# Folding the squares of two scan directions into one 128-row tile, in a bidirectional Mamba-2 layer with a feed-forward part

## The chip, the cores and the metric

The kernel runs on one core of one Trainium2 chip, in float32 throughout. The metric is the device time of one execution in microseconds (us). Five engines work side by side, each through its own queue in order: TensorE (PE; its weight loads are listed apart as PEld), VectorE (DVE), ScalarE (ACT), GpSimd (POOL) and SyncE (SP), which issues the DMAs.

## What is computed

Eight sequences of 512 tokens with 256 channels. Each is normalised, run through a Mamba-2 block forward and another one backward, projected and added to the input; then it is normalised again and goes through a dense layer with a low-rank correction. The part that matters here is the end of each Mamba-2 block, the gate, the mean of squares over the 512 inner channels of a token, and the output projection:

```python
def _mamba2(x, Win, convw, convb, dtb, Alog, Dsk, normw, Wout):
    ...
    y = jnp.transpose(ys, (1, 0, 2, 3)) + Dsk[None, None, :, None] * xs
    y = y.reshape(b, l, D_INNER)
    y = y * _silu(z)
    y = y * jax.lax.rsqrt(jnp.mean(y * y, axis=-1, keepdims=True) + 1e-05) * normw
    return y @ Wout
...
out_fwd = _mamba2(x, fWin, ...)
out_rev = jnp.flip(_mamba2(jnp.flip(x, axis=1), bWin, ...), axis=1)
out = jnp.concatenate([out_fwd, out_rev], axis=-1) @ Wo + bo
```

## The kernel before

**Tiling.** A sequence `b` (0 to 7) is cut into four chunks of 128 tokens. A `Pair(b, c)` works on two chunks at once: chunk `c` for the forward direction (`d` = 0) and chunk 3 - `c` for the backward one (`d` = 1). Channels lie on the 128 partitions, so a gated output `yg` of one direction is a tile of 128 partitions x 4 blocks x 128 tokens.

**The main loop** (L942 to L1123) makes one pass for each pair, 32 in all; the text calls them pass (b, c). In a pass `p` is the pair whose outputs are made, `q` the next pair, which is prepared, and `before` the one before. A pass also does convolution blocks of a later sequence (`work`, at most four), gates of a later pair (`gate`, `gate_silu`), and the output projection and feed-forward part (`Tail`, one a pass as a rule) of chunks that are complete. The order in which each engine does all this is written out by hand: at the end of each pass `pin()` fixes the instructions of every engine in the order in which they were issued. A wait in one queue therefore holds up everything behind it in that queue.

**One pass**, as far as the steps of the change are concerned:

- GpSimd: the scaling of the state (`decay_state`, L625), the scaling of the next pair's decays (`scale_c`, L558), `times_gate` for both directions (L676), four times `scale_x` (L591), two bias additions (L757, L719), `norm_power` (L696), and then `presum` (L702, L703), which adds the four blocks of squares of both directions down to one.
- ScalarE: the copies of the transposed inputs (`turn`, L582), `norm2` (L748), `tap` (L424), the copy in the tail's `turn` (L764), `norm_mean` of the pair before (L690), `square` for both directions (L679), in some passes `norm1` (L256), a late `silu` (L449), the gate's first `silu` (L501), `skip` (L615), more silus, the second `tap`, and the gate's second `silu`.
- TensorE: `outputs` (L635), `add_state` (L655), `turn` (L580), a `project` of `work` (L413), the tail's transposes (L762), `norm_sum` of the pair before (L685), half a gate (L493), `cb` (L601), `ffn` (L769), the output projection (L731), and more of L413 and L493.
- VectorE: `evict` (L669), `new_state` (L664), four scans (L569), `convolve` (L431), `mix` (L607), `add_ffn` (L772), `residual` (L738) and statistics (L225, L226).

In pass (1, 2), (3, 2) and (5, 2) VectorE also works out the step sizes of two sequences to come (class `Steps`, L333 to L358).

**The squares.** `square` writes the squares of one direction over that direction's gates in the tile `sz` (partitions x direction x block x half x tokens). `presum` adds blocks 2 and 3 to 0 and 1, then block 1 to 0. In the next pass `norm_sum` transposes the remaining 128 x 128 square of each direction on TensorE, so that tokens come to the partitions, and `norm_mean` sums along the 128 channels that are left, with a scaled and biased activation that accumulates; `norm_power` turns the two columns into the inverse root. The slots of the PSUM pools `p_tr` (two) and `p_proj` (three) go round in the order of use: the result of `norm_sum` and both results of `cb` are in `p_tr`.

In the last pass of a sequence (c = 3, `hold` in the code) the order differs: `norm_sum` comes between the two `turn`s, and ScalarE copies the second `turn` after `norm_mean`.

Of the kernel before, what the change touches and what calls it, by code (L numbers as in the profile page):

```python
# [8 lines left out]
F32 = mybir.dt.float32  # L9
AF = mybir.ActivationFunctionType  # L10
ALU = mybir.AluOpType
# [3 lines left out]
P = 128  # L15
NB, L, DM = 8, 512, 256
NC = L // P
DI = 512
# [8 lines left out]
EPS = 1e-5  # L27
# [4 lines left out]
def tile_bimamba_ffn(  # L32
# [39 lines left out]
    pe, dve, act, pool, sp = nc.tensor, nc.vector, nc.scalar, nc.gpsimd, nc.sync  # L72

    const = ctx.enter_context(tc.tile_pool(name="const", bufs=1))
# [13 lines left out]
    def ps(p, shape, name):  # L88
        return p.tile(shape, F32, name=name, tag=p.name)
# [60 lines left out]
    ident = const.tile([P, P], F32, name="ident")  # L150
# [3 lines left out]
    pool.memset(zeros, 0.0)  # L154
    neghalf = const.tile([P, NC], F32, name="neghalf")
    pool.memset(neghalf, -0.5)
    eps_col = const.tile([P, 1], F32, name="eps_col")
    pool.memset(eps_col, EPS / P)

    upto = const.tile([P, P + 1], F32, name="upto")  # L160
    pool.memset(upto, 1.0)
# [109 lines left out]
    def sm(name, b0, shape=(P, P), bufs=1):  # L271
        return small.tile(list(shape), F32, name=f"{name}_{b0}", tag=name, bufs=bufs)
# [103 lines left out]
    def steps_last(b0):  # L376
        g = seq[b0]["g"]
        last = g["last"] = sm("last", b0, (P, 64))
        act.activation(last[F], fold[F], AF.Copy, scale=upto[F, P:])
        act.activation(last[W], fold[W], AF.Copy, scale=onward[W, 0:1])  # L380
# [137 lines left out]
    class Pair:  # L518


        def __init__(self, b, c):
# [5 lines left out]
            self.r0 = [d * 64 + (n * NSG + self.s["i"]) * NH for d, n in enumerate(self.cn)]  # L527
            self.xdt, self.xw = {}, {}

        def tile(self, tag, shape, bufs=2, d=""):  # L530
            return chp.tile(list(shape), F32, name=f"{tag}_{self.name}_{d}", tag=tag, bufs=bufs)

# [143 lines left out]
            pool.tensor_tensor(yg, yg, m.gates(d), ALU.mult)  # L676

        def square(m, d):
            act.activation(m.gates(d), m.s["yg", d, m.cn[d]], AF.Square)  # L679

        def norm_sum(m):

            m.ss = ps(p_tr, [P, 2, P], f"ss_{m.name}")
            for d in range(2):
                pe.transpose(m.ss[:, d, :], m.gates(d)[:, 0, :], ident)  # L685

        def norm_mean(m):
            m.rs = small.tile([P, 2], F32, name=f"rms_{m.name}", tag="rms", bufs=8)
            for d in range(2):
                act.activation(  # L690
                    m.ss[:, d, :], m.ss[:, d, :], AF.Identity, bias=eps_col[:, 0:1], scale=1.0 / DI,
                    accum_out=m.rs[:, d:d + 1],
                )

        def norm_power(m):
# [2 lines left out]
                m.s["rs", d, m.cn[d]] = m.rs[:, d:d + 1]  # L698

        def presum(m):  # L700
            sq = m.s["gates", m.c // 2].sz[:, :, :, m.c % 2, :]
            pool.tensor_tensor(sq[:, :, :2], sq[:, :, :2], sq[:, :, 2:], ALU.add)  # L702
            pool.tensor_tensor(sq[:, :, 0], sq[:, :, 0], sq[:, :, 1], ALU.add)  # L703

    class Tail:

# [163 lines left out]
    gates = Gates(0, 0)  # L870
# [46 lines left out]
    def when(t, *what):  # L917
        for one in t if isinstance(t, list) else [t]:
            if one is not None:
                for w in what:  # L920
                    if w:
                        getattr(one, w)()
# [19 lines left out]
    for i in range(n):  # L942
        p, q = pairs[i], pairs.get(i + 1)
        b, c = order[i]
        t, t0 = begun(i), begun(i - 1)
        gates = None

        def gate(j):
            nonlocal gates
            if gates is None:  # L950
                gates = gated(i)
            if j < len(gates):
                gates[j][0](*gates[j][2:])

        def gate_silu(j):
            if j < len(gates):
                gates[j][1](*gates[j][2:])
# [50 lines left out]
        when(t0, "turn")  # L1008
        if not hold:
            when(before, "norm_sum", "norm_mean")  # L1010
        for d in range(2):
            p.square(d)
        if even and c in (1, 3) and ahead < NB:
            norm1(ahead + (c == 3))
        if not hold and b:
# [3 lines left out]
        if q:  # L1019
            if not hold or work[0] is not None:  # L1020
                gate(0)
            q.cb()
            gate_silu(0)
            if i == 0:
                steps_last(0)
            for d in range(2):
                q.scale_x(d)
        when(t0, "bias2")
# [154 lines left out]
```

## Time and profile before

| | us |
|---|---|
| three runs: lowest, median, highest | 618.14, 620.36, 621.55 |
| the profiled execution, its own time | 619.29 |
| its span, from the first to the last instruction | 617.5 |
| pass (1, 0), the first that the change touches, starts at | 119.43 |
| pass (6, 3), the last whose squares it touches, starts at | 533.34 |
| pass (7, 0) starts at | 546.87 |

All times inside the profile count from the start of the span. The profile adds up, for each engine, how long it was busy, follows the chain of work that ended last back from the end, and lists groups of instructions by line, each with its count, total and mean. A group's line also tells how long the engine was idle before these instructions and what ended the wait. TensorE's matmuls overlap, so its busy share says little; how far apart they start says more. The granted clock of TensorE is 0.993 of full speed over the span.

### The profile page before, as it was taken

Reading aid. Unit: us, or ns where it says so; the run is one execution under the profiler, and the core shown is the slowest. Engines: PE = TensorE matmul, PEld = TensorE weight load, DVE = VectorE, ACT = ScalarE, POOL = GpSimd, SP = SyncE. Lnnn points to the kernel's source line nnn. Section 1 sums busy time; section 2 is a strip of 40 time slices with the busy share of each in tenths; the row PEclk is TensorE's granted clock in tenths of the full one; section 3 lists DMA queues with packets and bytes.
Section 4 is the critical chain, followed back from the end, with each engine's and each line's share of the span. In section 5 each row is a group of like instructions: output and inputs, shape, how many; then the busy total and the mean of one; then the engine's idle time right before and its main releaser. Section 6 shows DMA issues by size and latency. Waiting matters only on the chain.

```text
span 617.5 us, 11937 instructions
## 1 busy us (share of the span) xinstructions
PE 596.7 (97%) x4316; PEld 428.3 (69%) x4316; DVE 545.9 (88%) x826; ACT 412.2 (67%) x949; POOL 460.9 (75%) x559
## 2 busy tenths in 40 slices
PE   5989999999999999999999999999999999999996
PEld 2467677677676776766767677767767767777784
DVE  5887988889999989988999998888999998888963
ACT  3688786867676576785786766775877755565531
POOL 3287885777857897776859799677967889499972
PEclk9999999999999999999999999999999999999998
DMA  7475340026064423108026422305206442444011
GB/s 223 139 227 197 111 106 7 2 83 192 4 197 153 120 86 102 37 5 257 19 84 186 129 73 86 121 20 189 54 6 191 120 120 87 121 120 120 18 52 35
DMA packets 36250, 64.80 MB, mean 105 GB/s; under 512 B 8608, under 2 KB 23392, under 8 KB 36192
## 3 DMA queue, kind: packets, MB, share of 16 engines
q1 hardware_dynamic: 34048, 64.00, 34.1%
q8 instruction: 34, 0.56, 0.4%
q10 hardware_dynamic: 2144, 0.04, 0.2%
q14 instruction: 24, 0.20, 0.1%
HBM read 59.12 MB, written 4.72 MB: 103 GB/s over the span
## 4 chain that ended last, share of the span: by engine, by line
PE 65%; DVE 19%; ACT 6%; POOL 5%; issue 3%; DMA 2%; SPq 0%; DVEq 0%; POOLq 0%; ACTq 0%
PE pp L413 16%; PE pm L731 12%; PE pz L493 12%; PE py L635 9%; DVE lam L569 5%; DVE xc L431 4%; PE pf L769 4%; PE pxs L580 4%; PE pst L655 2%; DVE lam L607 2%; DVE yg L669 1%; PE cb L601 1%; DVE x L738 1%; PE pz L510 1%; DMA dec__1431<-dec 1%
## 5 line engine op out<-in xcount | busy, mean ns | idle before, releaser
L431 DVE SCALAR_TENSOR_TENSOR xc<-pp,conv_sb,xc 128x511 f32<-128x511 f32 x180 | 133.4, 744 | 25.9 <-ACT xc L424 21.7
L413 PE MATMUL pp<-xhT,win_sb 128*128 128x512 f32 x320 | 151.5, 600 | 1.0 <-ACT v L278 0.5
L569 DVE TENSOR_TENSOR_SCAN lam<-lam,seed 128x512 f32<-128x512 f32 x128 | 145.6, 1197 | 0.0
L676 POOL TENSOR_TENSOR yg<-yg,sz 128x512 f32<-128x512 f32 x64 | 80.8, 1284 | 57.5 <-DVE yg L669 49.4
L731 PE MATMUL pm<-wy,yg 128*128 128x256 f32 x512 | 115.8, 379 | 0.0
L493 PE MATMUL pz<-xhT,win_sb 128*128 128x256 f32 x448 | 106.5, 380 | 0.3 <-DVE xc L431 0.2
L731 PEld LDWEIGHTS pm<-wy,yg 128*128 128x128 f32 x512 | 97.0, 190 | 13.4 <-issue 0.3
L493 PEld LDWEIGHTS pz<-xhT,win_sb 128*128 128x128 f32 x448 | 82.4, 190 | 17.9 <-issue 4.5
L413 PEld LDWEIGHTS pp<-xhT,win_sb 128*128 128x128 f32 x320 | 57.9, 192 | 47.1 <-issue 42.5
L615 ACT ACTIVATE yg<-xc,dcol 128x128 f32<-128x128 f32 x256 | 81.0, 393 | 0.0
L424 ACT ACTIVATE xc<-pp,conv_sb 128x512 f32<-128x512 f32 x64 | 49.7, 779 | 43.3 <-PE pp L413 43.2
L607 DVE TENSOR_TENSOR lam<-lam,cb 128x1024 f32<-128x1024 f32 x64 | 74.9, 1211 | 1.7 <-PE cb L601 1.7
L591 POOL TENSOR_TENSOR xdt<-xs,dw 128x512 f32<-128x512 f32 x64 | 66.6, 1045 | 1.1 <-ACT xs L582 1.1
L635 PE MATMUL py<-lam,xdt 128*64 128x128 f32 x1024 | 63.0, 276 | 0.6 <-POOL xs L591 0.6
L582 ACT COPY xs<-pxs 128x512 f32<-128x512 f32 x64 | 35.1, 588 | 39.8 <-PE pxs L580 39.8
L635 PEld LDWEIGHTS py<-lam,xdt 128*64 128x64 f32 x1024 | 55.3, 137 | 8.8 <-issue 2.5
L501 ACT ACTIVATE sz<-pz 128x512 f32<-128x512 f32 x56 | 33.1, 591 | 32.1 <-PE pz L493 31.9
L591 POOL TENSOR_TENSOR xs<-xs,dw 128x512 f32<-128x512 f32 x48 | 50.2, 1045 | 3.8
L669 DVE TENSOR_TENSOR yg<-py,yg 128x512 f32<-128x512 f32 x64 | 41.5, 682 | 9.2 <-PE py L635 5.0
L580 PEld LDWEIGHTS pxs<-ident,xc 128*128 128x128 f32 x256 | 28.2, 141 | 26.8 <-issue 13.4
L679 ACT ACTIVATE sz<-yg 128x512 f32<-128x512 f32 x64 | 38.0, 627 | 9.5 <-POOL yg L676 9.4
L702 POOL TENSOR_TENSOR sz<-sz 128x512 f32<-128x512 f32 x32 | 40.8, 1276 | 0.3 <-ACT sz L679 0.3
(234 smaller groups left out, 944.8 us busy)
## 6 DMA issues: line engine op xcount, KB each, us to landing
lam<-dat SPq DMA_DIRECT2D x64, 512.0 KB
x<-in_x_dram SPq DMA_DIRECT2D x36, 128.0 KB
out_dram<-x SPq DMA_DIRECT2D x32, 128.0 KB
x<-in_x_dram SPq DMA_DIRECT2D x7, 512.0 KB
win_sb<-in_win_dram SPq DMA_DIRECT2D x2, 640.0 KB
win_sb<-in_win_dram SPq DMA_DIRECT2D x2, 512.0 KB
wot<-in_wout_t_dram SPq DMA_DIRECT2D x2, 512.0 KB
v<-raw SPq DMA_DIRECT2D x48, 4.0 KB
```

What stands on the lines that cost most here:

```text
L413: pe.matmul(pp, lhsT=win_sb[:, d, k, c0:c0 + P], rhs=s["xhT"][:, k, :], start=(k == 0), stop=(k == NK - 1),)
L424: act.activation(self.acc, self.pp, AF.Identity, bias=self.w[:, 4:5], scale=self.w[:, 3:4])
L431: dve.scalar_tensor_tensor(self.acc[:, to], self.pp[:, of], self.w[:, 3 - j:4 - j], self.acc[:, to], ALU.mult, ALU.add,)
L493: pe.matmul(pz[:, j, :], lhsT=win_sb[:, d, k, blk * P:(blk + 1) * P], rhs=self.s["xhT"][:, k, cols], start=(k == 0), stop=(k == NK - 1),)
L569: dve.tensor_tensor_scan(lam, lam, sd, 0.0, ALU.mult, ALU.add)
L580: pe.transpose(pt[:, blk * P:(blk + 1) * P], m.s["xc", d][:, blk, m.tcol[d]], ident)
L591: pool.tensor_tensor(hb(to), hb(m.xw[d]), dw[:, j, cols].unsqueeze(2).to_broadcast([P, NH, HD]), ALU.mult)
L607: dve.tensor_tensor(m.lam[d], m.lam[d], m.pcb[d].unsqueeze(1).to_broadcast([P, NH, P]), ALU.mult)
L615: act.activation(yg[:, blk, :], m.s["xc", d][:, blk, m.tcol[d]], AF.Copy, scale=dcol[:, d, blk:blk + 1])
L635: pe.matmul(m.py[d][two * HD:(two + 1) * HD, blk, :], lhsT=lhsT, rhs=rhs, start=first, stop=last, skip_group_check=True,)
L676: pool.tensor_tensor(yg, yg, m.gates(d), ALU.mult)
L731: pe.matmul(t.pm[d], lhsT=yg[:, blk, :], rhs=wy[:, d, blk, :], start=(blk == 0), stop=(blk == NBLK - 1),)
```

## The change

The change concerns the sequences 1 to 6, which are called folded (`0 < b < NB - 1`); passes of the sequences 0 and 7 keep their code.

- `square` of a folded pair takes the 128 channel rows of a direction as two halves of 64 rows, and writes both halves to the same 64 rows of the tile: rows 0 to 63 for the forward direction, 64 to 127 for the backward one. The two halves lie where the tile kept the two directions. This makes four ScalarE instructions of 64 rows out of two of 128.
- The squares of a folded pair stand in ScalarE's queue after the gate's first `silu`, no longer right after `norm_mean`. Nothing is moved in the other queues, and no DMA is added, removed or moved.
- `presum` has a third addition, of one half to the other (128 x 128).
- `norm_sum` makes one transpose instead of two: its output has the forward direction in columns 0 to 63 and the backward one in columns 64 to 127. `norm_mean` sums 64 columns instead of 128, with a second constant for the bias.

```diff
-    eps_col = const.tile([P, 1], F32, name="eps_col")
-    pool.memset(eps_col, EPS / P)
+    eps_col = const.tile([P, 2], F32, name="eps_col")
+    pool.memset(eps_col[:, 0:1], EPS / P)
+    pool.memset(eps_col[:, 1:2], EPS / 64)
...
+            self.folded = 0 < b < NB - 1
...
         def square(m, d):
-            act.activation(m.gates(d), m.s["yg", d, m.cn[d]], AF.Square)
+            yg = m.s["yg", d, m.cn[d]]
+            if m.folded:
+                for j in range(2):
+                    act.activation(m.squares()[d * 64:(d + 1) * 64, j], yg[j * 64:(j + 1) * 64], AF.Square)
+            else:
+                act.activation(m.squares()[:, d], yg, AF.Square)
+
+        def squares(m):
+            return m.s["gates", m.c // 2].sz[:, :, :, m.c % 2, :]
 
         def norm_sum(m):
             m.ss = ps(p_tr, [P, 2, P], f"ss_{m.name}")
-            for d in range(2):
-                pe.transpose(m.ss[:, d, :], m.gates(d)[:, 0, :], ident)
+            for d in range(1 if m.folded else 2):
+                pe.transpose(m.ss[:, d, :], m.squares()[:, d, 0, :], ident)
 
         def norm_mean(m):
             m.rs = small.tile([P, 2], F32, name=f"rms_{m.name}", tag="rms", bufs=8)
             for d in range(2):
+                terms = m.ss[:, 0, d * 64:(d + 1) * 64] if m.folded else m.ss[:, d, :]
+                eps = eps_col[:, 1:2] if m.folded else eps_col[:, 0:1]
                 act.activation(
-                    m.ss[:, d, :], m.ss[:, d, :], AF.Identity, bias=eps_col[:, 0:1], scale=1.0 / DI,
-                    accum_out=m.rs[:, d:d + 1],
+                    terms, terms, AF.Identity, bias=eps, scale=1.0 / DI, accum_out=m.rs[:, d:d + 1]
                 )
...
         def presum(m):
-            sq = m.s["gates", m.c // 2].sz[:, :, :, m.c % 2, :]
+            sq = m.squares()
             pool.tensor_tensor(sq[:, :, :2], sq[:, :, :2], sq[:, :, 2:], ALU.add)
             pool.tensor_tensor(sq[:, :, 0], sq[:, :, 0], sq[:, :, 1], ALU.add)
+            if m.folded:
+                pool.tensor_tensor(sq[:, 0, 0], sq[:, 0, 0], sq[:, 1, 0], ALU.add)
...
             when(before, "norm_sum", "norm_mean")
-        for d in range(2):
-            p.square(d)
+        if not p.folded:
+            for d in range(2):
+                p.square(d)
...
             gate_silu(0)
             if i == 0:
                 steps_last(0)
+            if p.folded:
+                for d in range(2):
+                    p.square(d)
             for d in range(2):
                 q.scale_x(d)
```

## Prediction, made before the change was run

> **What bounds the kernel now.** First the page's busy times and its chain of work that ended last:
>
> ```profile
> PE 596.7 (97%) x4316; PEld 428.3 (69%) x4316; DVE 545.9 (88%) x826; ACT 412.2 (67%) x949; POOL 460.9 (75%) x559
> ...
> PE 65%; DVE 19%; ACT 6%; POOL 5%; issue 3%; DMA 2%; SPq 0%; DVEq 0%; POOLq 0%; ACTq 0%
> ```
>
> ScalarE, which gets most of the new work, has a third of the span free. TensorE leads the chain, but 35% of it lies elsewhere, so I read the chain in order of time (start, length, what). In pass (6, 2), as in most passes from (1, 3) on, it is TensorE without a hole:
>
> ```profile
> 520.86 0.22 PE pxt L762 x2
> 521.08 0.22 PE ss L685 x2
> 521.30 1.73 PE pz L493 x8
> 523.03 0.38 PE cb L601 x8
> ```
>
> A transpose of L685 takes 0.11 us of TensorE's queue. The eight matmuls after it take 1.73 us in every such pass, 0.216 each, so nothing waits there: TensorE is the bound. The Trainium skill (Perfetto Trace Analysis, Identifying the Most-Contended Engine) speaks against this reading: it takes weight-load share, not matmul share, as the measure of TensorE's headroom. By its rule the 69% would leave room and a transpose less might be worth nothing; the even spacing decides against it here.
>
> Around passes (1, 2), (3, 2) and (5, 2) it is different. VectorE, which has the step sizes of two sequences on top, runs without idle time from 284.29 to past 337, and TensorE waits for it at the end:
>
> ```profile
> 307.25 4.46 DVE lam L569 x4
> ...
> 320.55 0.76 DVE xc L431
> ...
> 321.39 0.64 ACT xc L449
> 322.03 0.04 issue
> 322.07 0.33 PE pxs L580
> ```
>
> The cause of part of this is in the timeline of pass (3, 2):
>
> ```profile
> 302.17 2.37 POOL L558 TENSOR_TENSOR dec__3137<-dec__3137,cc 128x1024 f32<-128x1024 f32 x1
> ...
> 303.70 0.99 DVE L343 SCALAR_TENSOR_TENSOR pzu<-r,e 128x128 f32<-128x128 f32 x1
> ```
>
> L343 takes 0.30 us at the start of the kernel but 1.57, 0.99 and 0.77 in these three passes, and each time it ends 0.15 us after GpSimd's L558 (160.41 against 160.25, 304.69 against 304.54, 448.75 against 448.60). So VectorE is held there until GpSimd has finished, though no semaphore ties the two. The Trainium skill (SBUF — State Buffer, SBUF: two separate sides) has the rule: a VectorE instruction with two SBUF inputs and a GpSimd instruction exclude each other from a shared port pair. The rule goes further than the trace: L335 has two SBUF inputs as well and took 0.29 us beside a GpSimd power (300.46, within 300.04 to 300.61). By the rule a later GpSimd could hold that one too, at up to 0.6 us in three passes, 1.7 us in all; by the row nothing. I leave it out.
>
> Last, in pass (6, 3) GpSimd leads the chain, with the very additions that the change extends:
>
> ```profile
> 546.12 1.26 POOL sz L702
> 547.38 0.07 issue
> 547.45 0.73 POOL sz L703
> 548.18 0.08 issue
> 548.26 0.20 POOL ln_rs L232
> ```
>
> **Part by part.** The rows for the prices (count, then busy us and mean ns):
>
> ```profile
> L702 POOL TENSOR_TENSOR sz<-sz 128x512 f32<-128x512 f32 x32 | 40.8, 1276 | 0.3 <-ACT sz L679 0.3
> L679 ACT ACTIVATE sz<-yg 128x512 f32<-128x512 f32 x64 | 38.0, 627 | 9.5 <-POOL yg L676 9.4
> L703 POOL TENSOR_TENSOR sz<-sz 128x256 f32<-128x256 f32 x32 | 23.4, 732 | 2.5
> L685 PE MATMUL ss<-ident,sz 128*128 128x128 f32 x64 | 12.5, 277 | 0.4
> L457 ACT ACTIVATE cc<-acc 64x512 f32<-64x512 f32 x16 | 10.0, 628 | 0.2
> ```
>
> *Transposes.* 24 are removed. Each is worth 0.11 us where TensorE leads (0.14 at most, the length of its weight load), 2.6 us in all; where another engine leads it is worth nothing. Lower bound zero: no reason for a loss.
>
> *Squares.* Half the rows save nothing: L457, 64 rows, takes 628 ns against 627. It costs a little more, since two of L679 start 0.52 us apart (two take 1.04, 219.04 to 220.08), while after L457 the next instruction starts only at its end, 0.64 later. So four cost 4 x 0.52 to 4 x 0.64; I take 2.56, the row of the same height, 1.5 us a pair above the 1.04 of before, 36 us of ScalarE over 24 pairs. What hides it is ScalarE's idle time before its next timed job. Queued behind the squares are `skip`, the silu of `work`, the second `tap` and the second gate silu. Idle time before those: 3.15 in (3, 0), 3.38 in (2, 2), 2.39 in the passes with c = 3 of odd sequences, 1.15 + 1.91 in (2, 0), 1.66 in (2, 3) and 1.20 in (2, 1). Only (2, 1) and (4, 1) are short, by about 0.3: the second gate's silu ends at 226.9 instead of 226.6, and its PSUM slot is not asked for again until well into the next pass. In (1, 1), (3, 1) and (5, 1) the squares push back the activations from which VectorE starts its step sizes: the last ends at 297.99, VectorE takes it at 299.17; 1.18 of the 1.5 fit and 0.35 comes out late, but L343 is being held for 0.69 longer than it needs anyway. So I cost the squares at nothing. Uncovered they would cost up to 36 us.
>
> The move itself takes the squares' wait for GpSimd (9.4 us in 17 places) off the gate's silu, which frees a PSUM slot sooner, but no matmul waits for that slot: nothing. `presum` now meets squares that are later: in (2, 2) they end at about 238.8 and GpSimd arrives at 238.98, in (2, 1) 224.6 and 225.52. It stays just covered; a miss of 0.1 would vanish in the GpSimd idle time that follows (2.44).
>
> *`norm_mean`* on 64 columns: the copies L764 (256 columns, 369 ns) and L582 (512, 588) give 0.86 ns a column, so 0 to 0.055 us off each of the two. It is followed by `cb`, which waits for nothing: nothing.
>
> *Third addition.* Not in the trace. From below: a line through L702 and L703 gives 2.1 ns a column and 460 ns at 128 (L373, 64 rows of 128 columns, has 457). From above: L703's 732. With the 0.08 us of waiting that each dependent pair shows, 0.54 to 0.81; I take 0.54, 13 us of GpSimd in all. In most passes idle GpSimd time follows (1.57, 2.44, 0.60, 3.57) and it costs nothing. It lands on the path in four places. In (1, 1), (3, 1) and (5, 1) `presum` runs straight on into L232, L625 and L558, which then releases L343 that much later: 0.54, 0.54, and in (5, 1) less 0.11 that GpSimd waits there for VectorE now. In (6, 3) the chain shown runs through it: 0.54.
>
> **Sum**, on the profiled execution's 619.29 (span 617.5 and 1.79 around it), stretch by stretch, since stages led by VectorE or GpSimd swallow the transposes in them:
> - to (1, 2): +0.54, nothing gained;
> - (1, 3) to (2, 3), five transposes before GpSimd's run to L558 starts: -0.55, then +0.54; what (3, 0) to (3, 2) save is swallowed;
> - (3, 3) to (4, 3) in the same way: -0.55 and +0.43;
> - (5, 3) to (6, 2): four, -0.44;
> - (6, 3): +0.54; (7, 0) makes the last folded transpose: -0.11.
>
> Together +0.40: 619.7 for that execution. The median of the runs lies 1.07 above it, so **620.8 us**. With the bounds: the addition at 0.81 gives +1.5, the fifteen transposes at 0.14 instead of 0.11 give -0.05. From the median of 620.36, and with half the spread of the three runs (1.7) on either side, the forecast's own range is 618.6 to 623.6. No change means within 0.5% (617.3 to 623.5), about what a measurement of this kernel can tell.
>
> **Rivals.**
> 1. *TensorE's saving in full.* If VectorE has more room than it looks and the GpSimd additions hide, 24 x 0.11 = 2.6: 617.7, at 0.14 617.0. For it: TensorE is seamless over most passes. Against: in (3, 3) the group of L635 lasts 3.19 us instead of 2.83 and the first four of L580 0.94 instead of 0.49, so TensorE already waits 0.8 there, and what it saved just before is lost. Chance 0.18.
> 2. *GpSimd becomes the bound* (the slower side). Place: the runs without idle time from 210 to 242 and from 354 to 385, where the addition delays L625 (margin to L664 0.66) and `times_gate`. If the delay is carried on from pass to pass, 24 x 0.54 = 13.0 less 2.6 gives 630.8; in half the passes, 13.0 / 2 - 2.6 = 3.9 gives 624.3. It decides once less than 0.54 idle GpSimd time is left in a pass. For it: 75% busy and digits of 9 in its slices; against: idle times of 1.6 to 3.6 after nearly every such run. Chance 0.20.
> 3. *ScalarE runs late*: squares nearer 0.78 each (L424, 128 x 512 with two pointer operands) would add 4 x 0.78 - 1.04 = 2.1 us a pair, 0.9 more than the idle time of (2, 1) and (4, 1) and 0.4 more than that of (2, 3) and (4, 3): 2.6 if none of it is caught later, 623.4. For it: L424 is the dearest row of this width. Against: its two pointer operands, which a square lacks. Chance 0.10.
>
> **How the numbers follow.** Forecast 0.52, nearly all of it within 0.5%; rival 1 lies at the edge, 0.10 beyond and 0.08 within; rival 2 0.17 beyond, 0.03 within; rival 3 half and half. So faster 0.12, same 0.65, slower 0.23. The range takes in rival 1 at 0.11 a transpose and rival 2 up to half the passes, 617.3 to 624.8; beyond lie some 0.1 on each side.
>
> **What would show it.** Right: L685 x40 with the pz group still 1.73 long, squares of folded pairs at 0.64 spacing with no TensorE or VectorE wait behind them, a third GpSimd addition near 0.46, L343 in (3, 2) and (5, 2) still ending 0.15 after L558, and the stall before L580 in (3, 3) larger by up to 0.6. Wrong: L343 back at 0.30, idle time of TensorE in passes (2, 0) to (2, 3), GpSimd without idle time over a whole sequence, or a cycle of eight passes (now 144.3 us, 192.89 to 337.16) that differs by more than 0.5 us.

## The result, and the profile after

| | before | after |
|---|---|---|
| runs side by side, median (lowest to highest), us | 619.75 (617.64 to 622.69), 22 runs | 621.28 (619.94 to 624.16), 22 runs |
| a second series, likewise | 619.94 (617.96 to 622.55), 35 runs | 621.55 (620.32 to 622.86), 12 runs |
| profiled execution, its own time (span) | 619.29 (617.5) | 622.07 (620.2); in the second series 620.32 (618.5) |

The ratio is 1.0028 [1.0014, 1.0041], and in the second series 1.0028 [1.0012, 1.0043]. The kernel is 1.5 us slower, less than the 0.5% that was called no change.

The page after, engine busy times and the chain that ended last:

```profile
PE 595.7 (96%) x4292; PEld 424.4 (68%) x4292; DVE 546.8 (88%) x826; ACT 443.2 (71%) x997; POOL 471.3 (76%) x584
...
PE 64%; DVE 16%; ACT 10%; POOL 5%; issue 3%; DMA 2%; ACTq 0%; DVEq 0%; POOLq 0%
```

TensorE has lost 24 transposes, ScalarE has 31 us more and 4% more of the chain. The groups of instructions that the change touches (count, then busy us, mean ns):

```profile
L687 ACT ACTIVATE sz<-yg 64x512 f32<-64x512 f32 x96 | 60.1, 626 | 0.9
L705 ACT ACTIVATE ss<-ss,eps_col 128x64 f32<-128x64 f32 (+1 forms) x64 | 19.6, 306 | 4.6 <-PE ss L698 3.5
L719 POOL TENSOR_TENSOR sz<-sz 128x128 f32<-128x128 f32 x24 | 11.0, 458 | 1.9
L698 PE MATMUL ss<-ident,sz 128*128 128x128 f32 x40 | 9.8, 279 | 0.4
```

The third addition takes 0.46 us, as predicted. In the chain of pass (6, 2) one transpose now stands between the tail's transposes and the gate, and the gate's group is as long as before, 1.73:

```profile
522.68 0.22 PE pxt L778 x2
522.89 0.11 PE ss L698
523.00 1.73 PE pz L495 x8
524.73 0.38 PE cb L605 x8
```

**Where the time went** is read by laying the two traces over each other: the start of each pass (the first matmul of `outputs`) after, less the same start before. In the first profile after, this difference falls by 0.11 in nearly every pass and jumps up in a few places:

```
(1,0) (1,3) (2,0) (2,3) (3,0) (3,2) (3,3) (4,3) (5,2) (5,3) (6,3) (7,0) (7,1)  end
+1.94 +1.97 +1.86 +1.64 +1.54 +1.32 +1.97 +1.64 +1.31 +2.10 +1.71 +1.59 +2.12 +2.74
```

The saw is the change at work: a transpose less per pass, and then +0.65 on the way to (3, 3), +0.79 to (5, 3) and +0.53 to (7, 1). From the start of (1, 0) to the start of (7, 1), the part of the program that the change touches and below called **the stretch**, it nets +0.19: 441.18 us before, 441.37 after, 441.41 in the second profile of after. What lies outside, 1.94 at the start and 0.62 in the tail, is taken up below.

At the jumps the chain shows the lock that the prediction spoke of, and now ScalarE ahead of it. The chain of passes (3, 1) to (3, 3):

```profile
295.39 0.63 ACT sz L687
296.03 0.63 ACT sz L687
...
300.43 0.32 ACT e L282
300.77 0.30 DVE pzu L335
...
305.56 1.02 issue
306.58 0.22 DVE dt L346
...
323.36 0.64 ACT xc L451
324.04 0.33 PE pxs L584
```

"issue" of 1.02 us between two VectorE instructions is the held L345. The timelines of GpSimd and VectorE in that pass (start, length):

```profile
301.20 0.46 POOL L719 TENSOR_TENSOR sz<-sz 128x128 f32<-128x128 f32 x1
...
304.14 2.37 POOL L562 TENSOR_TENSOR dec__3159<-dec__3159,cc 128x1024 f32<-128x1024 f32 x1
...
305.32 1.34 DVE L345 SCALAR_TENSOR_TENSOR pzu<-r,e 128x128 f32<-128x128 f32 x1
```

L345 took 1.90, 1.34 and 1.24 in (1, 2), (3, 2) and (5, 2), where L343 had taken 1.57, 0.99 and 0.77, and each time ends about 0.15 after L562. In (3, 2) TensorE feels it at its gates: counted from the pass's start, the first `pz` group begins 0.29 later than before, behind L347, which reads the last PSUM value of the step sizes, and the second 0.65 later.

In (1, 2) the product is held longer as well, yet (1, 3) starts only 0.03 later. There a DMA hides the cost: in (1, 1) GpSimd waits for the tile `dec`, and in the profile of before it came half a microsecond later than in the one of after:

```profile
142.23 2.36 POOL L558 TENSOR_TENSOR dec__1431<-dec__1431,cc 128x1024 f32<-128x1024 f32 x1 [5.85 <-DMA dec__1431<-dec]
```
```profile
143.66 2.36 POOL L562 TENSOR_TENSOR dec__1435<-dec__1435,cc 128x1024 f32<-128x1024 f32 x1 [5.35 <-DMA dec__1435<-dec]
```

GpSimd's wait there was 5.25 to 5.64 us in eleven of the fourteen profiles (in e10 and e11 another instruction ended it), 5.85 in before and 6.04 in e3 and e7. So it bears on every comparison with before; what comes behind (1, 3) is free of it. In (6, 3) the chain runs through the third addition:

```profile
547.82 1.26 POOL sz L716
549.07 0.07 issue
549.14 0.74 POOL sz L717
549.89 0.07 issue
549.95 0.46 POOL sz L719
550.42 0.08 issue
550.50 0.20 POOL ln_rs L234
```

### The profile page after: what moved, and what is told of

Its sections match the earlier page's. It is cut to its first block, busy times and chain, and to the rows that moved or that the text cites. A ratio compares the mean times of both kernels' runs of the same rounds, so it can differ in the third digit from the quotient of the medians.

```text
span 620.2 us, 11982 instructions
## 1 busy us (share of the span) xinstructions
PE 595.7 (96%) x4292; PEld 424.4 (68%) x4292; DVE 546.8 (88%) x826; ACT 443.2 (71%) x997; POOL 471.3 (76%) x584
## 4 chain that ended last, share of the span: by engine, by line
PE 64%; DVE 16%; ACT 10%; POOL 5%; issue 3%; DMA 2%; ACTq 0%; DVEq 0%; POOLq 0%
PE pp L415 16%; PE pm L747 12%; PE pz L495 11%; PE py L639 9%; PE pf L785 4%; PE pxs L584 4%; DVE lam L573 4%; DVE xc L433 3%; PE pst L659 2%; DVE r L344 1%; PE cb L605 1%; ACT yg L619 1%; ACT xc L426 1%; ACT xc L451 1%; DVE lam L611 1%
## 5 line engine op out<-in xcount | busy, mean ns | idle before, releaser
L415 PE MATMUL pp<-xhT,win_sb 128*128 128x512 f32 x320 | 153.2, 606 | 1.3 <-ACT xhT L814 0.7
L687 ACT ACTIVATE sz<-yg 64x512 f32<-64x512 f32 x96 | 60.1, 626 | 0.9
L584 PEld LDWEIGHTS pxs<-ident,xc 128*128 128x128 f32 x256 | 28.1, 141 | 27.4 <-issue 13.4
```

Of the source, the lines that this page charges most:

```text
L415: pe.matmul(pp, lhsT=win_sb[:, d, k, c0:c0 + P], rhs=s["xhT"][:, k, :], start=(k == 0), stop=(k == NK - 1),)
L687: act.activation(m.squares()[d * 64:(d + 1) * 64, j], yg[j * 64:(j + 1) * 64], AF.Square)
```

## The experiments

All were timed in five rounds against the kernel before; the stretch comes from the one profile of each, and the fourth column is the part of the difference that arises from the start of (1, 3) on. Line numbers are those of before or of after, as each builds on; in e1, e2 and e3 some are a few higher (their L626 and L559 are L625 and L558 of before).

| kernel | stretch, us | against before | of it from (1, 3) on | median, us | ratio to before |
|---|---|---|---|---|---|
| before | 441.18 | | | 619.66 to 620.46 | |
| after, after again | 441.37, 441.41 | +0.19, +0.23 | +0.15, +0.21 | 621.28, 621.55 | 1.0028, 1.0028 |
| e1 one transpose | 439.86 | -1.32 | -1.07 | 619.84 | 0.9999 [0.9982, 1.0016] |
| e2 third addition | 442.82 | +1.64 | +1.62 | 621.73 | 1.0031 [1.0017, 1.0045] |
| e3 half squares | 442.14 | +0.96 | +0.74 | 620.56 | 1.0007 [0.9988, 1.0025] |
| e4 before, no hold of L343 | 440.33 | -0.85 | -0.39 | 619.33 | 0.9987 [0.9969, 1.0004] |
| e5 after, four pairs unfolded | 439.55 | -1.63 | -1.21 | 618.94 | 0.9973 [0.9957, 0.9989] |
| e6 after, no hold of L345 | 441.01 | -0.17 | -0.08 | 620.73 | 1.0006 [0.9989, 1.0023] |
| e7 as e6, pair (6, 3) unfolded | 441.21 | +0.03 | -0.59 | 619.84 | 0.9997 [0.9981, 1.0013] |
| e9 before, steps free | 442.08 | +0.90 | +0.43 | 620.04 | 1.0009 [0.9992, 1.0027] |
| e10 as e7, steps free | 440.00 | -1.18 | -1.22 | 618.32 | 0.9977 [0.996, 0.9994] |
| e11 as e7, steps and slot free | 438.51 | -2.67 | -1.84 | 618.27 | 0.9966 [0.9948, 0.9983] |
| e12 before, steps and slot free | 439.08 | -2.10 | -0.74 | 617.20 | 0.9956 [0.9933, 0.9978] |

### The parts of the change, one by one

**e1, one transpose alone.** The second transpose of sequences 1 to 6 is left out; both means come from the first.

```diff
-            for d in range(2):
+            for d in range(1 if m.folded else 2):
                 pe.transpose(m.ss[:, d, :], m.gates(d)[:, 0, :], ident)
...
+                of = m.ss[:, 0 if m.folded else d, :]
```

> The kernel before with the second transpose of each pair in sequences 1 to 6 left out, nothing else changed (both means are then taken from the first transpose, so the backward direction's scale is not computed). Measured by the stretch from the start of pass (1, 0) to the start of pass (7, 1), 441.19 us before. My theory (0.11 us for each transpose where TensorE leads; those made in the passes with VectorE in the lead are swallowed): about 15 count, stretch shorter by 1.65 (1.4 to 1.9), and no gain from (3, 0) to (3, 2). Rival, TensorE's saving in full: 24 x 0.11 = 2.6 shorter. Rival, TensorE has headroom: 0.

The stretch fell by 1.32, a little less than the range: in steps of 0.10 to 0.11 a pass, with 0.09 given back on the way to (3, 3) and 0.31 to (5, 3). So a transpose is worth 0.11 where TensorE leads, and about half of the 24 are worth nothing. In (2, 3), (4, 3) and (6, 3) e1 gained nothing while after gains 0.10 to 0.11. There TensorE's second `turn` stands behind `norm_mean`, which e1 leaves at 128 columns and the change shortens from 346 to 293 ns twice; in (2, 3) the `turn`'s group takes 0.71 us in e1 and 0.60 in before and after.

**e2, the third addition alone**, 128 x 128, into a block that nobody reads.

```diff
+            if m.folded:
+                pool.tensor_tensor(sq[:, 0, 1], sq[:, 0, 0], sq[:, 1, 0], ALU.add)
```

> The kernel before with a third GpSimd addition of 128 x 128 in presum of sequences 1 to 6 (its result is not used; the outputs stay what they are). My theory (it counts only where GpSimd holds VectorE at L343 and in pass (6, 3)): the stretch from (1, 0) to (7, 1) longer by 0.54 + 0.54 + 0.43 + 0.54 = 2.05 (1.5 to 2.1), in four steps at (1, 2)-(1, 3), (3, 2)-(3, 3), (5, 2)-(5, 3) and (7, 0), and every other pass within 0.05. Rival, GpSimd becomes the bound: 4 to 13 longer, spread over the passes. Rival, the addition is hidden: 0.

+0.58 at (3, 3), +0.47 at (5, 3), +0.55 at (7, 1), and every other pass within 0.05: three of the four places named. The first of them, (1, 2), shows nothing: in (1, 1) GpSimd waits for a DMA (L558 for `dec`), 5.85 us in the profile of before and 5.30 in this one, and that difference hides the addition. An edit need not be behind such a difference: e6 and e7 run the same program up to there, and their waits are 5.37 and 6.04.

**e3, the squares alone**: four squares of 64 rows in place, behind the gate's silu.

```diff
-            act.activation(m.gates(d), m.s["yg", d, m.cn[d]], AF.Square)
...
+                for j in range(2):
+                    h = slice(j * 64, (j + 1) * 64)
+                    act.activation(m.gates(d)[h], yg[h], AF.Square)
...
```

> The kernel before with the squares of sequences 1 to 6 as four instructions of 64 rows, each half written where its own rows were, and issued after the gate's first silu as in the change; two transposes and two additions as before. My theory (ScalarE has the room): the stretch from (1, 0) to (7, 1) within 0.3 of 441.19, with VectorE starting its step sizes up to 0.4 later in (3, 2) and (5, 2) but L343 still ending 0.15 after L558. Rival, ScalarE runs late: 1 to 4 longer. Rival, the move of the squares helps: 0.3 to 1 shorter.

The stretch grew by 0.96, outside the 0.3 expected and short of the rival's 1 to 4: 0.20 at (1, 2), 0.10 at (3, 3) and 0.63 at (5, 3). The 0.20 is not the squares': `dec` came 0.19 later here than in before (a wait of 6.04 against 5.85), and e7, with the same 6.04, has (1, 2) 0.21 later too. That leaves 0.74 for the squares. The 0.10 goes through GpSimd, whose L626 took 1.14 us instead of 1.04 beside the product of L336. The timelines of VectorE and GpSimd in (5, 2):

```profile
447.10 1.02 DVE L336 TENSOR_TENSOR pzu<-e 128x128 f32<-128x128 f32 x1
```
```profile
446.89 1.08 POOL L626 TENSOR_TENSOR h__4701<-h__4517,tot 128x512 f32<-128x512 f32 x1
```

VectorE's step sizes begin late, behind the squares (L333 waits 0.20 for ScalarE), and so another product, e times e, comes to lie beside GpSimd's L626 and ends 0.15 after it: 1.02 us instead of 0.30. L343 behind it then takes 0.30.

**e1, e2 and e3 together.** Counted from (1, 3), where the landing of `dec` plays no part, e1 and e2 alone give -1.07 + 1.62 = +0.55, and the shorter `norm_mean` another -0.3: about +0.2, against +0.15 and +0.21 measured. At the jumps e1 and e2 give 0.67 and 0.78 where the change has 0.65 and 0.79. In the change the late squares therefore cost nothing more: the third addition holds L345 longer than they are late. Alone they cost 0.74.

**e5, the four dear pairs left in the old form.**

```diff
-            self.folded = 0 < b < NB - 1
+            self.folded = 0 < b < NB - 1 and (b, c) not in ((1, 1), (3, 1), (5, 1), (6, 3))
```

> The kernel after, but the pairs (1, 1), (3, 1), (5, 1) and (6, 3) keep the old form: two squares of 128 rows per pair at the old place, two transposes, no third addition. 20 pairs stay folded. Stretch means start of pass (1, 0) to start of pass (7, 1): 441.18 us before, 441.37 after. Theory (the third addition costs only where GpSimd's run ends in the instruction that releases the held VectorE product, and in (6, 3); the squares cost only where they delay the step sizes; both in exactly these four pairs): the jumps of +0.65 at (3, 3), +0.79 at (5, 3) and +0.53 at (7, 1) shrink to at most +0.3 each (what VectorE's stage swallows of the transposes saved just before), the 0.11 a pass elsewhere stays, so the stretch is 439.5 to 440.1, 1.1 to 1.7 below before; time 0.997 to 0.999 of before. Rival (additions or squares cost a little in every pass): the stretch falls by a sixth of the difference only, to 441.0 to 441.4, with the jumps still there.

The jumps shrank to 0.17, 0.31 and 0.09, the 0.11 a pass stayed, the stretch fell by 1.63. This kernel is faster than before by 0.27% [0.11, 0.43]. Laid against after, it gains 0.45 on the way to (1, 3), 0.49 to (3, 3), 0.48 to (5, 3) and 0.44 to (7, 1), and every other pass is the same within 0.01. So all of what the change costs inside the stretch sits in these four pairs, in nearly equal parts. The first of them counts as well: `dec` landed about alike in the two (waits of 5.46 and 5.35).

### The hold, and what stands behind it

**e4 and e6, L343 (L345 after) taken out of the hold**, in before and in after: reciprocal and the last step of the polynomial go to PSUM, so that each product has one input there. The edit of both:

```diff
-            dve.reciprocal(m.r, m.z)
-            dve.tensor_tensor(m.e, m.e, m.r, ALU.mult)
+            dve.reciprocal(m.z, m.z)
+            dve.tensor_tensor(m.e, m.e, m.z, ALU.mult)
...
-                dve.scalar_tensor_tensor(pol, pol, 1.0 / (2 * j + 1), u, ALU.add, ALU.mult)
-            dve.scalar_tensor_tensor(m.z, pol, 1.0, m.e, ALU.add, ALU.mult)
+                dve.scalar_tensor_tensor(pol if j > 1 else m.z, pol, 1.0 / (2 * j + 1), u, ALU.add, ALU.mult)
+            dve.scalar_tensor_tensor(m.z, m.z, 1.0, m.e, ALU.add, ALU.mult)
```

> The kernel before with the two products of the step sizes (L335 and L343) taking one input from PSUM instead of both from SBUF; same number of instructions, same outputs. My theory (VectorE is held at L343 by GpSimd's L558 because both its inputs lie in SBUF): L343 at 0.30 us in all passes instead of 1.57, 0.99 and 0.77, and the stretch from (1, 0) to (7, 1) shorter by 1.2 to 2.4 (0.69 + 0.47 at (3, 3) and (5, 3), up to 1.27 at (1, 3)). Rival, the length of L343 comes from something else (its output in PSUM, the queue): L343 stays at 0.8 to 1.6 and the stretch does not move.

> The kernel after, with the reciprocal, and the last step of the polynomial, of the step sizes written to PSUM, so that the products at L337 and L345 have one input in SBUF and one in PSUM. Theory (VectorE's product with two SBUF inputs is held by GpSimd's instruction, and the third addition and the late squares cost time through this alone in passes (1, 2), (3, 2), (5, 2)): L345 takes 0.30 in all of them, the jumps at (3, 3) and (5, 3) fall by 0.2 to 0.7 each; the stretch from (1, 0) to (7, 1) is 440.0 to 440.9, against 441.37 after. The jump of +0.53 at (7, 1) stays, since it is GpSimd's chain in (6, 3). Rival (VectorE itself, or GpSimd's next instruction, ends these passes whatever the product does): L345 at 0.30 but the stretch within 0.2 of 441.37.

The product took 0.30 us in all places, and yet e4 gained less than L343 had been held for and stayed below its range of 1.2 to 2.4, and e6 missed its range. The timelines of e6 in (3, 2):

```profile
303.48 2.37 POOL L562 TENSOR_TENSOR dec__3159<-dec__3159,cc 128x1024 f32<-128x1024 f32 x1
...
304.58 0.30 DVE L345 SCALAR_TENSOR_TENSOR pzu<-pzu,e 128x128 f32<-128x128 f32 x1
...
304.85 1.09 DVE L346 TENSOR_SCALAR dt<-v 128x128 f32<-128x128 f32 x1
```

The next instruction, L346, is now held instead: 1.79, 1.09 and 0.88 us in the three passes, 0.21 where it was free in after, and it ends 0.09 after L562. It has one input, but input and output are both in SBUF. In e4 the same instruction (L344) took 1.21, 0.62 and 0.41. In the sum the books balance: L343 was held for 1.27 + 0.69 + 0.47 = 2.43 in before, L344 for 1.00 + 0.41 + 0.20 = 1.61 in e4, which leaves a gain of 0.82, and 0.85 was measured. Place by place they do not: the hold fell by 0.27 or 0.28 in each, while 0.46, 0.21 and 0.19 were gained, the first with `dec` 0.28 earlier than in before. From (1, 3) on, 0.55 less hold brought 0.39.

**e7, as e6, and pair (6, 3) unfolded.**

> As the run before in this list, and pair (6, 3) keeps the old form (two transposes, no third addition). Theory: the jump of +0.53 at (7, 1) becomes 0 to +0.1 and nothing else moves: the stretch is 0.4 to 0.5 shorter than in that run, 439.5 to 440.5, time 0.996 to 0.999 of before. Rival (the jump at (7, 1) comes from the folded pair's late squares or from the DMAs of the outputs, not from the addition): the jump stays above +0.4.

At (7, 1) the jump of 0.53 became 0.13, so it was the addition. The stretch missed its range, because (1, 0) to (1, 3), where the program is that of e6, took 0.71 more: the wait of GpSimd for `dec` was 6.04 us here and 5.37 in e6. One DMA's landing can move the stretch by more than half a microsecond from run to run.

**e9 and e10, the whole chain of step sizes out of the hold**, in before and in the kernel of e7: the maximum and the product with A go to PSUM as well.

```diff
-            dve.scalar_tensor_tensor(m.z, pol, 1.0, m.e, ALU.add, ALU.mult)
-            dve.tensor_scalar(m.dt, m.v, 0.0, None, ALU.max)
-            dve.scalar_tensor_tensor(m.dt, m.z, 2.0, m.dt, ALU.mult, ALU.add)
-            dve.tensor_scalar(m.r, m.dt, a_col[:, 0:1], -1e30, ALU.mult, ALU.max)
...
+            dve.scalar_tensor_tensor(m.dt, m.z, 1.0, m.e, ALU.add, ALU.mult)
+            dve.tensor_scalar(m.u, m.v, 0.0, None, ALU.max)
+            dve.scalar_tensor_tensor(m.dt, m.dt, 2.0, m.u, ALU.mult, ALU.add)
+            dve.tensor_scalar(m.u, m.dt, a_col[:, 0:1], -1e30, ALU.mult, ALU.max)
...
-            act.activation(m.da, m.r, AF.Exp)
+            act.activation(m.da, m.u, AF.Exp)
```

> The kernel before, with the whole chain of step sizes kept off two SBUF operands: reciprocal, last polynomial step, the maximum and the product with A are written to PSUM, so that each instruction from L335 to L346 has an operand or its result there. Theory (GpSimd's L558 holds whichever VectorE instruction with SBUF on both sides comes next: with L343 freed, the maximum L344 was held in its place): every instruction of L335 to L346 takes 0.2 to 0.3 us in all four places, also in the kernel's start; the excess of L343 in before was 1.27, 0.69 and 0.47, so the stretch from (1, 0) to (7, 1) falls from 441.19 by 0.9 to 2.4, to 438.8 to 440.3. Rival 1 (VectorE's next instruction, the eviction of outputs, is held too): one of the next rows is longer by what was saved and the stretch stays above 440.2, as with the earlier form of this edit (440.33). Rival 2 (another engine ends these passes): rows short, stretch above 440.2.

> The kernel after, with pair (6, 3) in its old form and the same edit of the step sizes. Theory A (the hold is the only thing through which VectorE's stages swallowed the saved transposes and showed the third additions): 0.11 a pass from (1, 3) on without jumps at (3, 3) and (5, 3) above 0.2, 18 to 23 transposes in all: the stretch is 1.8 to 2.4 below that of the run before in this list. Theory B (VectorE ends the passes (3, 2) and (5, 2) by its own work, hold or no hold): jumps of 0.3 to 0.6 at (3, 3) and (5, 3), the stretch 0.8 to 1.6 below that of the run before. Rival (the late squares set the start of the step sizes): jumps above 0.6, the stretch less than 0.8 below.

Every instruction of the chain but the reciprocal took 0.27 to 0.36, and in (3, 2) VectorE was through with it 0.42 us earlier, counted from the pass's start, but e9's stretch grew by 0.90, where it was to fall by 0.9 to 2.4. TensorE had found a new wait, 1.16 us in e9 and, as its timeline shows, 1.54 in e10:

```profile
305.07 1.99 PE L495 MATMUL pz<-xhT,win_sb 128*128 128x256 f32 x8 [1.54 <-DVE h__3171 L668]
```

The step sizes now kept their PSUM slot until ScalarE's exponential had read it, in (3, 2) of e9 at 309.37, where in before the last reader, L345, was done at 305.14; and the gate had to take the slot that L668 (L664 in e9) frees. With TensorE made to lead in this way, e10 did lie 2.08 below e9, in the range of theory A, though 0.32 of it came on the way to (1, 3), where GpSimd's wait was 0.39 shorter than in e9, and jumps of 0.25 and 0.24 against e9 remained at (3, 3) and (5, 3). The next two runs take the new wait away.

**e11 and e12, as e10 and e9, with the slot freed**: the product with A and the exponential use SBUF again.

> As the kernel after with the step sizes free (pair (6, 3) in its old form), but the last of the VectorE instructions (the product with A, L348) writes to SBUF again and ScalarE's exponential reads it there. In that run TensorE's gate (pz) waited 1.54 us in (3, 2) for L668, since the slot of the step sizes was held until the exponential, some 6 us later than in before. Theory (a wait for a PSUM slot had taken the place of the hold): the wait goes, the pz group starts within 0.1 us of the transpose before it in (1, 2), (3, 2) and (5, 2), L348 stays at 0.3 us (a pointer operand; 0.29 in before), and the stretch from (1, 0) to (7, 1) falls from 440.00 to 436 to 438.5; time 0.990 to 0.996 of before. Rival (VectorE still ends these passes): TensorE waits as long at the next convolution or transpose instead, the stretch stays above 439.

> The same edit of the step sizes on the kernel before. Theory (with the hold and the slot gone, TensorE leads all passes, and the change is worth its transposes): the stretch falls from 442.08 to 438 to 441, the run above lies 1.8 to 2.6 us below this one. Rival (the third additions and late squares show up in another wait once TensorE has caught up with GpSimd): less than 1.2 us between the two.

In e11 the gate follows the transpose at once:

```profile
304.19 0.27 PE L698 MATMUL ss<-ident,sz 128*128 128x128 f32 x1
304.30 1.89 PE L495 MATMUL pz<-xhT,win_sb 128*128 128x256 f32 x8
```

These two have the lowest medians of the study. e11's stretch lies at the edge of its range (438.51 against at most 438.5) and e12's within its own, but the two stand only 0.57 apart, where theory had 1.8 to 2.6 and the rival less than 1.2. Pass by pass, e11 gains 1.70 on e12 in steps of a transpose and loses 1.13 again. The largest loss, 0.64 on the way to (1, 3), has a hold behind it after all: in (1, 2) L348 was still held, 1.10 us in e11 and 0.52 in e12 (its L346), since the third addition lets L562 end later. Another 0.21 is lost from (3, 2) to (4, 0), 0.19 from (5, 2) to (6, 0) and 0.09 at (7, 1). The chain of e11 from (3, 2) to (3, 3) shows the second:

```profile
297.92 0.32 ACT e L282
298.27 0.30 DVE pzu L335
...
304.03 1.27 DVE yg L673 x2
305.31 0.60 DVE h__3171 L668
305.90 4.46 DVE lam L573 x4
...
319.99 0.04 issue
320.04 0.64 ACT xc L451
320.68 0.04 issue
320.72 0.33 PE pxs L584
```

With no hold in (3, 2), VectorE works without a hole from the step sizes to the last convolution block, and TensorE waits for it at L584; what the transposes saved while VectorE led is lost there. The first step size itself, L335, waits for ScalarE's `e`, behind the late squares: it starts 0.77 after the pass in e11, while in e12 VectorE comes to it from its own work at 0.48. So with the hold gone the late squares have a part in this loss, and no run separates the two. From (1, 3) on the change is worth 1.10 here. The medians of e11 and e12 cannot be told apart by their intervals.

### What lies outside the stretch

**e8, the kernel after once more**, for its profile.

> The kernel after, unchanged, once more, for the profile. Theory (the stretch from (1, 0) to (7, 1) is set by the program; the start before (1, 0) and the tail behind (7, 1) scatter with the clock and with the DMAs): the stretch is 441.2 to 441.6 again, while the start of (1, 0) lies anywhere from 119.4 to 121.5 and the tail from 56.2 to 60.6; the ratio of times is 1.000 to 1.004. Rival (the change itself makes the start later, by 1.9 us): the start of (1, 0) is 121.2 to 121.5 again.

Pass (1, 0) started at 119.54, 0.10 later than before, with the stretch at 441.41. So the 1.94 us at the start of the first profile are not the change's. They go with the clock: the first projections, before and after, in TensorE's timeline,

```profile
9.09 6.83 PE L413 MATMUL pp<-xhT,win_sb 128*128 128x512 f32 x12 [0.46 <-ACT xhT L798]
```
```profile
9.40 8.06 PE L415 MATMUL pp<-xhT,win_sb 128*128 128x512 f32 x11 [0.66 <-ACT xhT L814]
```

ran at 0.86 us a matmul until full clock was granted, and at 0.43 from then on; it was granted at 12.0 in before, at 15.6 in after, at 11.9 in e8.

e8 has the same clock record as the profile of before (full from 12, half from 76.8 to 80.2, half again from 612.7), and its span is 1.00 longer: 0.10 at the start, 0.23 in the stretch, 0.67 in the tail, where no line was changed. There SyncE's queue loads two chunks of x, and the second load waits for a store. SyncE's waits in the tail of before and of e8 (us in total, times, longest), and the chain of e8 in its tail:

```profile
SPq L716 <- DMA out_dram<-x: 0.8, 1, 0.8
```
```profile
SPq L732 <- DMA out_dram<-x: 2.1, 1, 2.1
```
```profile
596.38 2.96 DMA out_dram<-x
...
599.36 1.97 DMA x<-in_x_dram
...
601.49 0.73 POOL x L735
```

The wait of 0.8 is 2.1 in e8, where store and load lead the chain. The store took longer where a fetch of program code (16 KB, one packet in the DMA records of kind instruction) fell between 0 and 2 us behind the store's issue: at 597.21 in e8, with the store at 596.38. Of the fourteen profiles of this study the six with such a fetch (after, e8, e1, e6, e7, e10) have 2.8 to 3.8 us for the issue of the two loads, and the eight without have 1.6 to 1.7. That fetch comes 31.7 to 31.9 us behind the start of (7, 1) in the six kernels that make all transposes, and 34.8 to 38.9 in the eight profiles of kernels that leave some out. It goes with the transposes left out and not with the length of the whole program: e2 and e3, which add instructions for GpSimd and ScalarE, keep it at 31.8. That TensorE then needs its next block of code later is the likely reason, not a shown one. That the change moved a code fetch into a store is what these numbers say. In e8 the transposes behind that load start 0.39 later for it; the other 0.28 of the tail come with the last group of matmuls, L785, 2.09 instead of 1.78 us, which lies under the half clock. No run moved the fetch alone.

## Why the prediction held, point by point

Of the signs that the prediction named, most came true: L685 (L698) 40 times with the `pz` group at 1.73, squares 0.64 apart, an addition of 0.46, the product's end 0.15 behind the scaling, and eight passes as long as before. Two did not. The stall before L580 in (3, 3) did not grow (0.94 us in both); TensorE had waited before, at the gates of (3, 2). And VectorE does wait behind the squares: the chain of after has ScalarE ahead of L335.

The stretches of the sum, as predicted and as the first profile has them:

| stretch | predicted | measured |
|---|---|---|
| (1, 0) to (1, 3) | +0.54 | +0.03 |
| (1, 3) to (3, 3) | -0.01 | 0.00 |
| (3, 3) to (5, 3) | -0.12 | +0.13 |
| (5, 3) to (6, 3) | -0.44 | -0.39 |
| (6, 3) to (7, 1) | +0.43 | +0.41 |
| sum | +0.40 | +0.19 (differences rounded) |

- *Transposes* at 0.11, where TensorE leads: right (e1). 15 were counted as gained; 13 show up as steps in the profile after, since (2, 0) and (4, 0) give none: the tail's transposes come 0.11 later there. Of the 0.25 missed between (3, 3) and (5, 3) 0.11 is this; about as much is that one transpose more than the three of (5, 0) to (5, 2) was swallowed there (e1 too gives 0.31 back), and 0.04 the addition (0.47 in e2).
- *Third addition* at 0.46 + 0.08, free but for four places: right for three (e2, e5). The first place was predicted at +0.54 and shows +0.03. The cost is there, 0.45 by e5; what the sum lacked is that the start of GpSimd's run in (1, 2) hangs on the landing of `dec`, 0.5 us earlier in both profiles of after. The chain of before has this DMA in it.
- *Squares* at 0.64 each and hidden: right for the change as a whole. The reason given, that L343 is held anyway, is what e3 shows from the other side: without the third addition 0.74 comes out, 0.63 of it through a product that the prediction did not name.
- *`norm_mean`* at nothing: its size was right (0.053 off each, within 0 to 0.055), but 0.1 is gained in each of (2, 3), (4, 3) and (6, 3), where TensorE's second `turn` stands behind it.
- *The rule of the Trainium skill* (SBUF — State Buffer, SBUF: two separate sides) was carried to L343 alone and L335 left out, on a row that did not speak: L335 ended 0.14 after the power beside it, so 0.29 us was all that it could take. After, in (1, 2), the same product took 0.48 (157.05 to 157.53) beside the third addition (156.92 to 157.38). e3 shows the rule at L336. The same page (Who interferes with whom) says that an instruction of one input contends as well when it runs in a mode that uses both ports, and names tensor_scalar: L346 in e6 agrees, 1.09 instead of 0.21.
- *Rival 1* (the full 2.6) falls with the saw: the hold takes part of it, and where the hold is gone VectorE's stages still do (e11 against e12). The stall quoted against it is rather 0.7 than 0.8: in (2, 3), a pass of the same kind, L635's group takes 2.94 us, not 2.83. *Rival 2* (GpSimd bound) falls: the eight passes from (2, 0) to (4, 0) took 144.28 against 144.27. *Rival 3* falls at 0.64 a square.
- *The whole*: +0.40 was predicted and 1.5 measured, 0.9 to 2.5 by the interval. In the profiles the stretch accounts for 0.2 and the tail, which the prediction had at nothing, for 0.62 and 0.67. With `dec` landing in before as it did in after, the stretch of before would be some 0.5 shorter and the change would cost about 0.7 in it; this is an estimate from e6 and e7, where 0.67 in the landing made 0.70. Together with the tail that would nearly be the 1.5, but no run settles it.
- *Luck*: that 620.8 came within 0.5 of the 621.28 measured is partly luck. The three runs that it started from have a median of 620.36, and the 22 later ones 619.75, so that the base was 0.6 too high and the difference 1.1 too low. Within the stretch, +0.40 against +0.19 is also the sum of misses in both directions, -0.51 in the first row and +0.25 in the third.

## What to carry to other kernels

A saving on the engine that leads most of the chain can be lost again in part at each stage that another engine ends (in e1 0.09 and 0.31 of some 0.5 each); so lay the pass starts of two traces over each other and look for the jumps, then undo the change at the jumps alone (e5: 4 pairs of 24 turned 0.28% slower into 0.27% faster). Before a difference is put down to an edit, see whether a DMA landed alike in both traces; the landing of `dec` alone made 0.7 us between e6 and e7. Where VectorE is held by GpSimd, freeing one instruction hands the hold to the next one with SBUF on both sides, and a PSUM operand that ends a hold can keep a slot for which TensorE then waits: look at all of the chain, and at who takes the slot next.

## What the hardware showed that was not expected

- The hold is regular and not bound to one kind of instruction: with two SBUF inputs VectorE's instruction ended 0.14 to 0.16 us after GpSimd's (L343, L345, L337, and L336 in e3), with one SBUF input and an SBUF output 0.08 to 0.09 after (L344, L346, L348).
- TensorE started at half speed (0.86 us a matmul against 0.43 later), and full clock was granted at 11.9 to 15.6 us of the span, run by run; (1, 0) started at 118.6 to 121.4 in fourteen profiles. Later half-clock spells of 3.4 us came at 77, at 580 to 588 or at both, in some runs only.
- Where a code fetch of 16 KB fell into a store of 128 KB, the load that waits for this store was issued 1.2 to 2.2 us later than elsewhere (six profiles against eight).
- Squares of 64 rows follow each other at 0.64 us, those of 128 rows at 0.52, with the same mean length of 0.63.
